# Third Strassen product by a second step, z added straight onto x1's buffer, and layer norm's squares on ScalarE: a two-layer graph kernel

## The chip, the cores and the metric

The kernel runs on one core of a Trainium2 chip. The metric is the device time of one launch in microseconds (us), the median of several runs. A core has five engines that run side by side: TensorE (PE, matrix products, into PSUM), VectorE (DVE), ScalarE (ACT), GpSimd (POOL) and SyncE (SP), which here issues the DMAs.

## The reference

64 graphs of 256 nodes with 512 features, two layers, everything in fp32:

```python
# layer 0:  x = layernorm(x + relu([x, (adj @ x) / max(deg, eps)] @ W.T))
# layer 1:  x = layernorm(x + softmax(w)[:, None] * (x @ Wv)),
#           w = q . (adj @ (k * mask)) / sqrt(512) * mask,  q, k = split(x @ Wqk)
def _layernorm(x, axis=-1, eps=1e-5):
    m = jnp.mean(x, axis=axis, keepdims=True)
    v = jnp.var(x, axis=axis, keepdims=True)
    return (x - m) / jnp.sqrt(v + eps)
```

(cut and joined; `deg` is the sum of a row of `adj`.) The kernel rewrites layer 0 as `x @ W_left` plus `adj @ (x @ W_right)` scaled by 1/deg, and folds Wq and Wk into one 512x512 matrix before the loop, so each layer has one product of x with 512x1024 weights and one product of adj with a 256x512 matrix (the "gather").

## The kernel before

Two graphs make a pair, j = 0 to 31. Iteration j works on layer 0 of pair j and, between its steps, on layer 1 of pair j-1. The product with the weights is done by a Strassen (Winograd) scheme with seven products P1 to P7; P1, P2 and P5 are themselves done by a second Strassen step of seven smaller products (`inner`), the others by plain accumulated matmuls (`outer`, `pairs`). All pieces are cut into units, and the program's order on TensorE is a string of unit names.

```python
    def inner(p, X, sides, w, q, done=lambda fifth: None):
        [...]
        lo, hi = w[:, :HF], w[:, HF:]              # two halves of a PSUM bank; HF = 256
        def first_two():
            mm(hi, s(0), b["T1"], start=True)
            mm(lo, X.chunk(block, 0, 0), b["B11"])
            act.copy(q[0][:, :HF], lo)
            tick()
        def second():
            mm(lo, s(1), b["T2"])                  # accumulates on lo: after the copy has read it
            act.copy(q[0][:, HF:], lo)
            tick()
        def third():
            mm(lo, s(2), b["T3"])
            act.copy(q[1].rearrange("p (h f) -> p h f", h=2), lo[:, None, :].to_broadcast([P, 2, HF]))
            fifth.append(small.tile([P, HF], F32, name="fifth", bufs=3))
            act.copy(fifth[0], hi)
            mm(q[0][:, :HF], X.chunk(block, 0, 1), b["B21"])
            tick()
        def last_two():
            mm(q[1][:, :HF], X.chunk(block, 1, 1), b["T4"])
            mm(q[0][:, HF:], s(3), b["B22"])
            [...]
```

Four calls of `inner`'s list are four steps: two matmuls, one, two, two. Side work (norms, softmax, sums for the next pair) is put in lists, `chains`; `tick()` at the end of each unit takes from them what fits by a clock that counts 0.43 or 0.86 us for each matmul and an assumed cost for each VectorE and ScalarE instruction. The clock does not know of DMAs. So each engine's order is fixed when the program is built.

```python
    def tick():
        while not quiet[0]:
            for c in list(chains):
                if c[2][0] <= clock[0] and c[3][0][0].free <= clock[0] + room[c[3][0][0]]:
                    step(c)
                    break
            else:
                return
[...]
    def degrees(j):
        [...]
        def degree(k, t):                           # r: the rows of adj, tile "turn"
            act.activation(r[:, k, t], r[:, k, t], AF.Copy, accum_out=deg[:, k, t:t + 1])
```

The tile `turn` has one buffer. It holds in turn the 32x32 blocks of x1 on their way through DMAs into the transposed `x1T`, and the rows of adj of the next pair, of which `degrees` makes the sums. `place` issues the 16 DMAs for x1T once the last norm of the pair before is done, then x and the rows are loaded by the same queue.

Of the kernel before, what the change touches and what calls it, by code (L numbers as in the profile page):

```python
# [50 lines left out]
class Side:  # L52
# [3 lines left out]
    def __init__(self, pool, name, home=None):  # L56
        self.pool, self.name = pool, name
        home = pool.tile([P, 2 * N_SIDE], F32, name=name) if home is None else home
        self.a = home.rearrange("p (k u e v n) -> p k u e v n", k=2, u=2, e=2, v=2)
        self.s = self.i = None  # L60

    def open_sums(self):
        self.s = self.pool.tile([P, 2, 4, 2, P], F32, name=self.name + "_s")
        self.i = self.pool.tile([P, 4, 3, P], F32, name=self.name + "_i")

    def block(self, s, ks):
        return self.s[:, ks, s] if isinstance(s, int) else self.a[:, ks, s[0], :, s[1]]

    def chunk(self, s, k, e):
        return self.s[:, k, s, e] if isinstance(s, int) else self.a[:, k, s[0], e, s[1]]  # L70
# [24 lines left out]
def resnorm_kernel(  # L95
# [104 lines left out]
    def load_xT(j, home=None):  # L200
        Xs[j] = Side(pool, "xT", home)
# [54 lines left out]
    def weight_sums(w, name):  # L256
# [4 lines left out]
        it = const.tile([P, 3, 3, HF], F32, name=f"{name}i")  # L261
        sides = {"B22": b22, "T2": t2, "T3": b12, "T4": t4}
        sub = lambda *args: lambda: vec.tensor_sub(*args)

        def inner_of(n, p, b):
# [5 lines left out]
                + [sub(b12, b22, b12), sub(t4, b21, t2)] + inner_of(1, "P2", b21))  # L271
# [3 lines left out]
    def outer_sums(X, eng, ks=slice(0, 2)):  # L275
        if X.s is None:
# [4 lines left out]
                (eng, lambda: eng.tensor_sub(a(S3), a(A11), a(A21))),  # L281
                (eng, lambda: eng.tensor_sub(a(S4), a(A12), a(S2)))]
# [5 lines left out]
    def inner_sums(X, eng, part):  # L288
# [3 lines left out]
        ks, b = ((slice(0, 2), X.first_row), (slice(2, 3), lambda k, e: X.s[:, k, S1:S1 + 1, e]))[part]  # L292
# [36 lines left out]
    def inner(p, X, sides, w, q, done=lambda fifth: None):  # L329

        n, block = {"P1": (0, A11), "P2": (1, A12), "P5": (2, S1)}[p]
# [25 lines left out]
        def last_two():  # L357
            mm(q[1][:, :HF], X.chunk(block, 1, 1), b["T4"])
            mm(q[0][:, HF:], s(3), b["B22"])
            if p != "P2":  # L360
# [30 lines left out]
    def gather(a, w, dst, u, p5, p2):  # L391
        r11, r12, r21, r22 = (dst[:, :, t, h * HF:(h + 1) * HF] for t in range(NT) for h in range(2))
# [8 lines left out]
        def u1():  # L401
            twice(u, "A11", "B11")
            act.copy(r11, of(u))
            tick()

        def g2():
            twice(p2, "A12", "B21")
            vec.tensor_add(r11, of(p2), r11)
# [22 lines left out]
        def u4():  # L431
            twice(u, "A22", "T4", start=False)
            act.copy(r21, of(u))
            tick()
        return dict(a=[u1], b=[g2], c=[g5], d=[u2], e=[u3], f=[g3], g=[u4])


# [21 lines left out]
    def norm0(j):  # L459
# [4 lines left out]
        x1Ts[j] = Side(pool, "x1T")  # L464
        sq = []

        def scaled(k, t):
            o = own[:, k, t]
            vec.scalar_tensor_tensor(o, z[:, k, t], rdeg[:, k, t:t + 1], o, op0=OP.mult, op1=OP.add)

        def residual(k, t):
            o = own[:, k, t]
            vec.scalar_tensor_tensor(o, o, 0.0, xs[j][:, k, t], op0=OP.max, op1=OP.add)
# [14 lines left out]
        for k in range(2):  # L488
            mv = small.tile([P, NT, 2], F32, name="mv")
            stats, scale = layer_norm(own[:, k], mv, NT)  # L490
# [396 lines left out]
```

## Time and profile before

| | |
|---|---|
| time, median of 3 | 1900.72 us (1900.2 to 1901.08) |
| span of the profiled run | 1898.0 us |
| ScalarE copies bank to bank, 128x256 / 128x512 | 384 of 363 ns / 192 of 585 ns |
| ScalarE scaling of the norms, 128x512 | 256 of 808 ns |
| VectorE norm statistics, 128x512, and their aggregate | 256 of 676 ns and 256 of 182 ns |
| VectorE adds bank + SBUF, 128x512 | about 680 ns |
| GpSimd sums for x and x1 | 0.45 to 1.6 us |

The page gives the busy time of each engine and the chain of work that ended last. Lists of groups give one line for each kind of instruction with its count, busy time and mean. A timeline line has start, duration, engine, source line, operation, output and input, shape and count; brackets give the idle time before it and what ended it. All instructions are recorded through two helper lines (L90 and L173), so tiles tell them apart. TensorE runs each fp32 matmul as two passes, so a count of x2 is one matmul.

### The profile page before, as it was taken

What the parts mean: (1) busy time and instruction counts of PE and PEld (TensorE: products, weight loads), DVE (VectorE), ACT (ScalarE), POOL (GpSimd) and SP (SyncE); (2) the same over time, 40 slices, a digit from 0 to 9 for tenths busy, and PEclk for the clock granted to TensorE, in tenths of its full rate; (3) what the DMA queues carried; (4) which work ended last, traced back from release to release, by engine and by line L of the source; (5) the groups of instructions that cost most, each with busy time, mean ns of one, the idle gap of its engine ahead of it and who ended that gap; (6) DMA issues with size and microseconds to landing.
All of it is one profiled execution on the core that took longest, in us unless ns stands there. A gap on an engine that the chain in (4) does not pass through costs nothing.

```text
span 1898.0 us, 22655 instructions
## 1 busy us (share of the span) xinstructions
PE 1875.2 (99%) x6596; PEld 1246.5 (66%) x6596; DVE 1588.2 (84%) x2952; ACT 1061.1 (56%) x2571; POOL 752.3 (40%) x898
## 2 busy tenths in 40 slices
PE   9999999999999999999999999999999999999997
PEld 5656666667666666666676666666666666666764
DVE  7788988888987889888889888898888898888886
ACT  3546555556555565554565655655555656555654
POOL 4444423444324434235444244343244442344421
PEclk9999999999999999999999999999999999999999
DMA  6333343442343433443433434334434334344321
GB/s 223 78 73 80 96 104 92 99 117 74 100 107 73 117 82 96 104 96 92 118 75 97 106 74 116 86 98 107 103 76 117 80 94 106 85 105 106 82 58 51
DMA packets 389147, 182.17 MB, mean 96 GB/s; under 512 B 272160, under 2 KB 353696, under 8 KB 389024
## 3 DMA queue, kind: packets, MB, share of 16 engines
q1 hardware_dynamic: 389024, 180.72, 36.7%
q8 instruction: 54, 0.88, 0.2%
q14 instruction: 69, 0.57, 0.1%
HBM read 114.10 MB, written 34.06 MB: 78 GB/s over the span
## 4 chain that ended last, share of the span: by engine, by line
PE 91%; DVE 4%; DMA 1%; SPq 1%; POOL 1%; issue 1%; ACT 0%; ACTq 0%; DVEq 0%; POOLq 0%
PE bank L173 91%; DVE own L90 1%; SPq L178 1%; DMA w<-w_t 1%; DVE st L90 1%; DVE y L90 0%; DVE tv L90 0%; DMA xT<-x_t 0%; DVE t_i L90 0%; DVE bank L90 0%; POOL xT_i L90 0%; POOL sa L90 0%; ACT own L90 0%; DMA turn<-adj 0%; POOL xT_s L90 0%
## 5 line engine op out<-in xcount | busy, mean ns | idle before, releaser
L90 ACT COPY bank<-bank 128x256 f32<-128x256 f32 (+1 forms) x576 | 252.0, 437 | 240.4 <-PE bank L173 231.4
L90 POOL TENSOR_TENSOR xT_i<-xT 128x256 f32<-128x256 f32 x62 | 58.9, 950 | 524.5 <-DMA xT<-x_t 490.0
L173 PE MATMUL bank<-w,x1T_s 128*128 128x512 f32 x512 | 260.4, 592 | 0.0
L173 PE MATMUL bank<-w,xT_s 128*128 128x512 f32 x512 | 230.2, 592 | 1.0 <-DVE y L90 1.0
L90 POOL TENSOR_TENSOR x1T_i<-x1T 128x256 f32<-128x256 f32 x64 | 51.2, 799 | 396.9 <-DMA x1T<-turn 383.0
L90 ACT ACTIVATE own<-own,shift,rstd 128x512 f32<-128x512 f32 x256 | 197.7, 808 | 14.1 <-DVE shift L90 13.8
L173 PE MATMUL bank<-tv,sa 128*128 128x256 f32 x768 | 191.9, 379 | 0.0
L173 PEld LDWEIGHTS bank<-tv,sa 128*128 128x128 f32 x768 | 145.8, 190 | 47.4 <-issue 16.0
L90 ACT COPY y<-bank 128x512 f32<-128x512 f32 x192 | 109.0, 587 | 119.9 <-PE bank L173 116.5
L90 DVE TENSOR_TENSOR y<-bank,y 128x512 f32<-128x512 f32 x192 | 128.5, 683 | 56.7 <-ACT y L90 53.0
L90 DVE BATCH_NORM_STATS2 st<-own 128x6 f32<-128x512 f32 x256 | 173.0, 676 | 2.4
L173 PE MATMUL bank<-t,xT_s 128*128 128x512 f32 (+1 forms) x384 | 158.6, 522 | 2.9 <-ACT own L90 2.9
L173 PEld LDWEIGHTS bank<-w,xT_s 128*128 128x128 f32 x512 | 97.2, 190 | 96.4 <-issue 85.8
L173 PE MATMUL bank<-t,x1T_s 128*128 128x512 f32 (+1 forms) x384 | 158.2, 521 | 0.3 <-ACT y L90 0.3
L90 ACT ACTIVATE turn<-turn 128x256 f32<-128x256 f32 x128 | 52.6, 411 | 169.2 <-DMA turn<-adj 169.2
L90 DVE TENSOR_TENSOR bank<-bank,fifth 128x256 f32<-128x256 f32 x256 | 97.0, 425 | 41.8 <-PE bank L173 41.8
L90 ACT COPY agg<-bank 128x512 f32<-128x512 f32 x128 | 74.4, 581 | 95.3 <-PE bank L173 94.0
L173 PE MATMUL bank<-t,x1T 128*128 128x512 f32 x256 | 125.2, 592 | 0.0
L173 PE MATMUL bank<-t,xT 128*128 128x512 f32 x248 | 121.6, 592 | 0.0
L90 POOL TENSOR_TENSOR sa<-adj 128x256 f32<-128x256 f32 x128 | 108.7, 849 | 26.8 <-ACT adj L90 20.9
L173 PE MATMUL bank<-t_i,x1T_i 128*128 128x256 f32 x384 | 114.4, 380 | 0.7 <-POOL x1T_i L90 0.4
L173 PE MATMUL bank<-t_i,xT_i 128*128 128x256 f32 x384 | 114.5, 380 | 0.2
(144 smaller groups left out, 4171.3 us busy)
## 6 DMA issues: line engine op xcount, KB each, us to landing
x<-x SPq DMA_DIRECT2D x64, 512.0 KB, 4.7
xT<-x_t SPq DMA_DIRECT2D x62, 512.0 KB, 6.2
x1T<-turn SPq DMA_DIRECT2D x496, 64.0 KB, 2.3
out<-own SPq DMA_DIRECT2D x62, 512.0 KB, 5.0
adj<-adj_t SPq DMA_DIRECT2D x64, 256.0 KB, 2.9
turn<-adj SPq DMA_DIRECT2D x64, 256.0 KB, 4.9
row<-d SPq DMA_DIRECT2D x31, 256.0 KB, 4.9
wqk<-wqk_t SPq DMA_DIRECT2D x4, 512.0 KB, 5.5
```

Source lines behind the costliest of these rows:

```text
L90: return self.tc.keep_in_program_order(getattr(self.engine, name)(out, *args, **kwargs))
L173: tc.keep_in_program_order(nc.tensor.matmul(ps, a, b, start=start, stop=True, skip_group_check=True))
L178: return tc.keep_in_program_order(nc.sync.dma_start(out, in_))
```

## The change

Three things are changed together. First, P3 of both layers is done by `inner` as well. It works on the sum S4, whose own small sums have to be made (`fourth_sums`, on GpSimd), whose result starts afresh in the PSUM banks y, so that what stood in y is added to the output before, and which has a fifth term to add afterwards. To save SBUF, S4 lies in the slot of a sum that is no longer read (S1 in layer 0, S2 in layer 1). Second, half of the gathered z of layer 0 is multiplied by 1/deg and added onto `own` (which becomes x1) straight from PSUM by VectorE; the tile z is half as large. Third, the norm's mean comes from an accumulated sum of the VectorE operation before it, and the variance from a Square with accumulation on ScalarE, in place of VectorE's statistics. The order strings are changed to fit. The core of the diff:

```diff
@@ -53,21 +52,22 @@
 
 
 
-    def __init__(self, pool, name, home=None):
+    def __init__(self, pool, name, over, home=None):
         self.pool, self.name = pool, name
+        self.slot = (0, 1, 2, over)
         home = pool.tile([P, 2 * N_SIDE], F32, name=name) if home is None else home
         self.a = home.rearrange("p (k u e v n) -> p k u e v n", k=2, u=2, e=2, v=2)
         self.s = self.i = None
 
     def open_sums(self):
-        self.s = self.pool.tile([P, 2, 4, 2, P], F32, name=self.name + "_s")
+        self.s = self.pool.tile([P, 2, 3, 2, P], F32, name=self.name + "_s")
         self.i = self.pool.tile([P, 4, 3, P], F32, name=self.name + "_i")
 
     def block(self, s, ks):
-        return self.s[:, ks, s] if isinstance(s, int) else self.a[:, ks, s[0], :, s[1]]
+        return self.s[:, ks, self.slot[s]] if isinstance(s, int) else self.a[:, ks, s[0], :, s[1]]
 
     def chunk(self, s, k, e):
-        return self.s[:, k, s, e] if isinstance(s, int) else self.a[:, k, s[0], e, s[1]]
+        return self.s[:, k, self.slot[s], e] if isinstance(s, int) else self.a[:, k, s[0], e, s[1]]
 
     def first_row(self, k, e):
 
[...]
@@ -278,8 +278,13 @@
         a = lambda s: X.block(s, ks)
         return [(eng, lambda: eng.tensor_add(a(S1), a(A21), a(A22))),
                 (eng, lambda: eng.tensor_sub(a(S2), a(S1), a(A11))),
-                (eng, lambda: eng.tensor_sub(a(S3), a(A11), a(A21))),
-                (eng, lambda: eng.tensor_sub(a(S4), a(A12), a(S2)))]
+                (eng, lambda: eng.tensor_sub(a(S3), a(A11), a(A21)))]
+
+    def fourth_sums(X):
+
+        ks = slice(0, 2)
+        gp.tensor_sub(X.block(S4, ks), X.block(A12, ks), X.block(S2, ks))
+        inner_sums(X, gp, 2)
 
     def run_now(steps):
         for _, work in steps:
[...]
@@ -328,7 +334,7 @@
 
     def inner(p, X, sides, w, q, done=lambda fifth: None):
 
-        n, block = {"P1": (0, A11), "P2": (1, A12), "P5": (2, S1)}[p]
+        n, block = {"P1": (0, A11), "P2": (1, A12), "P5": (2, S1), "P3": (0, S4)}[p]
         b = sides[p]
         s = lambda r: X.i[:, r, n]
         lo, hi = w[:, :HF], w[:, HF:]
[...]
@@ -357,7 +363,7 @@
         def last_two():
             mm(q[1][:, :HF], X.chunk(block, 1, 1), b["T4"])
             mm(q[0][:, HF:], s(3), b["B22"])
-            if p != "P2":
+            if p in ("P1", "P5"):
                 for k in range(2):
                     vec.tensor_add(q[k][:, HF:], q[k][:, HF:], fifth[0])
             done(fifth[0])
[...]
@@ -388,8 +394,18 @@
         vec.tensor_sub(t4, b21, t2)
         return {"B11": b11, "B21": b21, "B22": b22, "T1": t1, "T2": t2, "T3": t3, "T4": t4}
 
-    def gather(a, w, dst, u, p5, p2):
-        r11, r12, r21, r22 = (dst[:, :, t, h * HF:(h + 1) * HF] for t in range(NT) for h in range(2))
+    def gather(a, w, dst, u, p5, p2, own=None, rdeg=None):
+
+        if own is None:
+            r11, r12, r21, r22 = (dst[:, :, t, h * HF:(h + 1) * HF] for t in range(NT) for h in range(2))
+        else:
+            r12, r22 = dst[:, :, 0], dst[:, :, 1]
+
+        def onto(t, ps):
+            for k in range(2):
+                r = own[:, k, t, :HF]
+                vec.scalar_tensor_tensor(r, ps[:, k * HF:(k + 1) * HF], rdeg[:, k, t:t + 1], r,
+                                         op0=OP.mult, op1=OP.add)
 
         def twice(ps, s, b, start=True):
             for k in range(2):
[...]
@@ -430,10 +452,36 @@
 
         def u4():
             twice(u, "A22", "T4", start=False)
-            act.copy(r21, of(u))
+            if own is None:
+                act.copy(r21, of(u))
+            else:
+                onto(1, u)
             tick()
         return dict(a=[u1], b=[g2], c=[g5], d=[u2], e=[u3], f=[g3], g=[u4])
 
+
+    def norm_of(src, total):
+
+        rstd, shift, less, var = (small.tile([P, NT], F32, name=x) for x in ("rstd", "shift", "less", "var"))
+
+        def mean():
+            vec.tensor_scalar(less, total, -1.0 / F, None, op0=OP.mult)
+
+        def square(t):
+            junk = small.tile([P, F], BF16, name="junk", bufs=1)
+            act.activation(junk, src[:, t], AF.Square, bias=less[:, t:t + 1], accum_out=var[:, t:t + 1])
+
+        def factor():
+            act.activation(rstd, var, AF.Ln, bias=eps, scale=1.0 / F)
+            act.activation(rstd, rstd, AF.Exp, scale=-0.5)
+
+        def shifts():
+            vec.tensor_tensor(shift, less, rstd, op=OP.mult)
+
+        def scale(t):
+            act.activation(src[:, t], src[:, t], AF.Identity, bias=shift[:, t:t + 1], scale=rstd[:, t:t + 1])
+        return [(vec, mean)] + [(act, lambda t=t: square(t)) for t in range(NT)] + [(act, factor), (vec, shifts)] + [
+            (act, lambda t=t: scale(t)) for t in range(NT)]
 
     def layer_norm(src, mv, n):
 
[...]
@@ -486,13 +535,13 @@
                      sq[0][a * Q:(a + 1) * Q, b].rearrange("p k c t q -> p (k c t) q"))
         places[0] = place
         for k in range(2):
-            mv = small.tile([P, NT, 2], F32, name="mv")
-            stats, scale = layer_norm(own[:, k], mv, NT)
+            total = small.tile([P, NT], F32, name="sum")
             work = []
             for t in range(NT):
-                work += [(vec, lambda k=k, t=t: scaled(k, t)), (vec, lambda k=k, t=t: residual(k, t)), stats[t]]
+                work += [(vec, lambda k=k, t=t: scaled(k, t)),
+                         (vec, lambda k=k, t=t, total=total: residual(k, t, total))]
             turns = [(vec, lambda k=k, t=t: turn(k, t)) for t in range(NT)] if j < NP - 1 else []
-            queue(1, "norm", *work, *scale, *turns)
+            queue(1, "norm", *work, *norm_of(own[:, k], total), *turns)
 
     def scale_scores(j, to):
         vec.scalar_tensor_tensor(to, scores.pop(j), inv_scale, mask_sb[:, 2 * j:2 * j + 2, :],
[...]
@@ -601,8 +652,11 @@
         def after_p4(k):
             act.copy(own[:, k, 1], u[k])
 
-        def after_p3(k):
-            vec.tensor_add(yt[:, k, 0], y[k], yt[:, k, 0])
+        def after_p3(fifth):
+            for k in range(2):
+                vec.tensor_add(yt[:, k, 0], y[k], yt[:, k, 0])
+            add_fifth(yt[:, :, 0, HF:], fifth)
+
         def after_p5(fifth):
             pass
         return after_p1, after_p2, after_p3, after_p4, after_p5, after_p6, after_p7
[...]
@@ -632,7 +686,8 @@
 
         def after_p5(fifth):
             for k in range(2):
-                vec.tensor_add(vs[j][k][:, 1], y[k], vs[j][k][:, 1])
+                for t in (1, 0):
+                    vec.tensor_add(vs[j][k][:, t], y[k], vs[j][k][:, t])
 
         def after_agg():
             for k in range(2):
[...]
@@ -641,8 +696,11 @@
         def after_p4(k):
             dot(u[k], k, 1)
 
-        def after_p3(k):
-            vec.tensor_add(vs[j][k][:, 0], y[k], vs[j][k][:, 0])
+        def after_p3(fifth):
+            for k in range(2):
+                v = vs[j][k][:, 0]
+                vec.tensor_add(v, y[k], v)
+                vec.tensor_add(v[:, HF:], v[:, HF:], fifth)
         return after_p1, after_p2, after_p3, after_p4, after_p5, after_p6, after_p7, after_agg
 
     def pairs(ps, X, slot, b, done):
[...]
@@ -685,24 +744,27 @@
         k = inner("P5", X, W0, pw[1], y, a5)
         m = inner("P2", X, W0, pw[0], o, a2)
         p, q = pairs(u, X, S2, W0["T2"], a6), pairs(u, X, S3, W0["T3"], a7)
-        r, s = pairs(y, X, S4, W0["B22"], a3), pairs(u, X, A22, W0["T4"], a4)
+        r, s = inner("P3", X, W0, pw[1], y, a3), pairs(u, X, A22, W0["T4"], a4)
         if j == 0:
             run("i k i k i k i k", i=i, k=k)
             flush("degrees")
             load_rows(1)
         elif j == 1:
             run("i k i k i k i k", i=i, k=k)
+            fourth_sums(X)
             run("m p p m p p m", m=m, p=p)
             flush("norm")
             places[0](range(16))
         else:
-            run("i f k", i=i, k=k, f=open1)
+            run("i k", i=i, k=k)
             send_scores(j - 2)
-            run("i f k", i=i, k=k, f=open1)
+            run("i l k", i=i, k=k, l=open1)
             flush("norm")
             fetch_scores(j - 2)
             places[0](range(16))
-            run("i f k i f k", i=i, k=k, f=open1)
+            run("i k i k", i=i, k=k)
+        if j != 1:
+            fourth_sums(X)
         if j > 0:
             flush("mask")
             sumsM[j - 1] = adj_sums(j - 1)
[...]
@@ -714,51 +776,49 @@
             shared[0] = 1.0
         if j != 1:
             run("m p p m p p m", m=m, p=p)
-        run("q q q q m", m=m, q=q)
+        run("q q q", q=q)
+        flush("w0")
+        run("r q r m r s r", m=m, q=q, r=r, s=s)
         if j > 0:
             Y = x1Ts.pop(j - 1)
             inner_sums(Y, gp, 0)
             sums_Y = (*outer_sums(Y, vec), (vec, lambda: inner_sums(Y, gp, 1)))
         if j > 1:
             queue(1, "sums", *sums_Y)
-        run("r r r r", r=r)
         T = sums_T(ys[j])
 
         if j != 1 and j < NP - 1:
             degrees(j + 1)
-        zs[j] = pool.tile([P, 2, NT, F], F32, name="z")
-        g = gather(sumsA.pop(j), T, zs[j], pw[1], y[1], y[0])
-
-        def load_next():
+        zs[j] = pool.tile([P, 2, NT, HF], F32, name="z")
+        g = gather(sumsA.pop(j), T, zs[j], pw[1], y[1], y[0], owns[j], rdegs[j])
+
+        def sums_next():
             if j == NP - 1:
                 return
-            if j > 0:
-                load_xT(j + 1)
-                shared[0] = 1.25
             inner_sums(Xs[j + 1], gp, 0)
             rest = outer_sums(Xs[j + 1], gp)
             run_now(rest[:1])
             inner_sums(Xs[j + 1], gp, 1)
             late_sums.extend(rest[1:])
         if j == 0:
-            load_next()
+            sums_next()
             held = [c for c in chains if c[1] == "w1"]
             chains[:] = [c for c in chains if c[1] != "w1"]
-            run("s s a b c d s e s g f", s=s, **g)
+            run("s s s a b c d e g f", s=s, **g)
         else:
             u2, o2, y2 = o, pf, y
             b1, b2, b3, b4, b5, b6, b7, b8 = layer1(j - 1, ys[j][:, :, 0], o2, u2, y2)
             jj = inner("P1", Y, W1, pw[0], u2)
             k = inner("P2", Y, W1, y[0], o2, b2)
             if j == 1:
-                run("s s a b c d s e s g f", s=s, **g)
+                run("s s s a b c d e g f", s=s, **g)
                 flush("w1")
                 queue(1, "sums", *sums_Y)
                 run("j k j k j k j", j=jj, k=k)
                 b1(None)
                 run("k", k=k)
             else:
-                run("s s j a b s j c d s j e k j", s=s, j=jj, k=k, **g)
+                run("s s j s a b j c d j k e j", s=s, j=jj, k=k, **g)
                 quiet[0] = True
                 run("k", k=k)
                 quiet[0] = False
[...]
@@ -773,18 +833,22 @@
             g = gather(sumsM.pop(j - 1), T, aggs[j - 1], pw[0], o2[1], o2[0])
             h, q = pairs(u2, Y, S2, W1["T2"], b6), pairs(u2, Y, S3, W1["T3"], b7)
             n = inner("P5", Y, W1, pw[1], y2, b5)
-            p, open1 = pairs(u2, Y, A22, W1["T4"], b4), pairs(y2, Y, S4, W1["B22"], b3)
+            p, open1 = pairs(u2, Y, A22, W1["T4"], b4), inner("P3", Y, W1, pw[1], y2, b3)
             norm0(j)
             mask_adj(j)
             run("k h h" if j > 1 else "h h", k=k, h=h)
             if j == 1:
                 degrees(2)
                 flush("degrees")
-            load_next()
-            run("n k" if j > 1 else "n", k=k, n=n)
-            run("h h a n b q d q n c q e q p n g p f p", h=h, n=n, q=q, p=p, **g)
+            if j < NP - 1:
+                load_xT(j + 1)
+            run("n k h h" if j > 1 else "n h h", k=k, n=n, h=h)
+            fourth_sums(Y)
+            shared[0] = 1.25
+            sums_next()
+            run("a n b q d q n c q e q n p g f", n=n, q=q, p=p, **g)
             b8()
-            run("p", p=p)
+            run("p l p l p l", p=p, l=open1)
             py, pu = pu, py
         else:
             norm0(0)
[...]
```

Left out: the sums of b22 for P3 among the weights' sums (four more per layer, once), the same two steps of `onto` in g2, the same norm at layer 1's end, and the last pair behind the loop, whose P3 becomes `inner` in the same way.

## The prediction

> **What bounds the kernel now.** I read the page's busy shares first, then its chain that ended last, then ScalarE's waits, then the timeline of one pair of graphs.
>
> ```profile
> PE 1875.2 (99%) x6596; PEld 1246.5 (66%) x6596; DVE 1588.2 (84%) x2952; ACT 1061.1 (56%) x2571; POOL 752.3 (40%) x898
> ...
> PE 91%; DVE 4%; DMA 1%; SPq 1%; POOL 1%; issue 1%; ACT 0%; ACTq 0%; DVEq 0%; POOLq 0%
> ```
>
> TensorE is busy for 99% of the span and carries 91% of the chain; the others are hidden. In the timeline a 256-column matmul takes 0.43 us to the next one and a 512-column one 0.86, so I count in units of 0.431 us (256 columns). One pair j in the middle is 134 units, 57.8 us; the timeline agrees: from 171.5 to 1732.5 us there are 27 pairs, 57.8 us each. TensorE therefore has no slack to lose, and every engine that it waits for counts at once. Where is that nearest?
>
> ```profile
> ACT turn L90 <- DMA turn<-adj: 169.2, 29, 7.0
> ```
>
> This line of ScalarE's waits says: 29 times, once for each pair from 2 to 30, ScalarE stands still for 5.8 us on average until the rows for the degree sums land. Its queue is in order, so a PSUM copy queued behind them stands too. The timeline shows what follows (the pair at 576 us, TensorE then ScalarE):
>
> ```profile
> 603.36 1.02 PE L173 MATMUL bank<-t,xT 128*128 128x512 f32 x2
> 604.78 0.67 PE L173 MATMUL bank<-t_i,x1T_i 128*128 128x256 f32 x2 [0.40 <-POOL x1T_i L90]
> ...
> 602.58 0.42 ACT L90 ACTIVATE turn<-turn 128x256 f32<-128x256 f32 x1 [7.04 <-DMA turn<-adj]
> 602.90 0.19 ACT L90 ACTIVATION_READ_ACCUMULATOR turn<-turn 128x1 f32 x1
> 603.00 0.40 ACT L90 ACTIVATE turn<-turn 128x256 f32<-128x256 f32 x1
> 603.30 0.19 ACT L90 ACTIVATION_READ_ACCUMULATOR turn<-turn 128x1 f32 x1
> 603.39 0.56 ACT L90 COPY own<-bank 128x512 f32<-128x512 f32 x1
> 603.86 0.42 ACT L90 ACTIVATE turn<-turn 128x256 f32<-128x256 f32 x1
> 604.18 0.19 ACT L90 ACTIVATION_READ_ACCUMULATOR turn<-turn 128x1 f32 x1
> 604.27 0.37 ACT L90 COPY bank<-bank 128x256 f32<-128x256 f32 x1
> ```
>
> The second step of layer 1's P1 (604.78) overwrites the half bank that the copy at 604.27 empties, and starts 0.14 us after that copy's end at 604.64. The profile names GpSimd as the releaser, but in two other pairs (257.60 and 720.64 us) the same matmul also starts 0.14 us after the same copy, with GpSimd still busy. Call L the start of the first degree sum, measured from the pair's first matmul. Over the 29 pairs L is 24.0 to 26.5, mean 25.2. The copy ends at L + 2.1; TensorE wanted it at 28.0. So only pairs with L over 25.8 stall, and by tenths: three do. The kernel before sits just short of an edge.
>
> **What the Trainium skill says.** "PSUM — Partial Sum Buffer", section "Engine vs sequencer instructions": ScalarE's and VectorE's queues are strict FIFO. The stretch above agrees (the copy of a bank long full waited for the DMA). "ScalarE: Activation LUTs", section "What ACT_TABLE_LOAD costs": an ACTIVATE takes 186 ns + 0.833 ns per element of a row, about 93 ns more for each per-partition pointer operand, and neighbours overlap by about 93 ns. The trace agrees: the norm's scaling with two pointers should be 799 ns and is 808, the mask with one 492 against 514. "SBUF — State Buffer", section "SBUF: two separate sides": a VectorE operation with two SBUF inputs and a GpSimd one lock each other out. The trace fits: y times agg, both in SBUF, takes 685 to 1745 ns, bank times agg about 690.
>
> **The change, part by part.**
> *TensorE.* P3 was 4 matmuls of 512 columns = 8 units; as an inner product it is 7 of 256 = 7 units. Two layers, 32 pairs: 64 x 0.431 = 27.6 us less. A pair becomes 132 units, 56.9 us. Alone this makes 1873 us, and no other part of the change can take more from the chain.
> *ScalarE.* Squares: 252 of 128x512 with one pointer, an estimate from that page 186 + 93 + 427 = 706 ns, plus an accumulator read of 0.19 (as behind turn): +226 us. Inner copies: 128 x 0.363 + 64 x 0.585 + 64 x 0.375 = +108. Half of z no longer copied: 64 x 0.588 = -38. Sum +296, so 1357 us, 73%.
> *VectorE.* Statistics gone: 252 x (0.676 + 0.182) = -216. Accumulator reads of the 252 sums +35. z straight from the bank: 192 x about 0.4 = +77; then shorter scaling, fewer z adds and no S4: about -45 - 24 - 23. The product P3 starts afresh, so the earlier y must be added first: 64 y and 62 v adds x 0.683 = +86, and its fifth term +44. Sum near -66, about 1520 us, 81%.
> *GpSimd.* S4 (33 x 1.4) and 256 small sums of 0.5 to 0.9: about +200, so 950 us, 51%.
> On shares alone all of this is hidden. The waits decide.
>
> *The stretch around L in the new order.* From the order strings, a pair with j > 1 runs: i k i l k i k i k = 16 units; m p p m p p m = 13; q q q = 6; r q r m r s r = 13; s s j s a b j c d j k = 21; then e. The first j ends after 54 units, 23.3 us; the second wants to start after 60, at 25.9 (before: 28.0). TensorE comes here two microseconds earlier because three of four closing P3 steps went to the end of the pair before, one s moved up and P3 shrank. L does not move with it: it hangs on the last transposes of x1, 18 us earlier (582.54 to 583.25 in the timeline, 7.1 us after the first matmul), on 16 transposing DMAs, the x load and the load of the rows, all in the same order as before. I allow 0.2 us and take L = 25.0.
> ScalarE's stream there reads, in the changed program: turn turn turn, copy of j's first half bank, turn, own, square square, Ln Exp, copy of j's second, square square, copy of d (z). The new squares stand between copies that TensorE waits for. With steps from the timeline above (turn with its read 0.41, 256 copy 0.30 to the next start, 512 copy 0.50) and, for squares, 0.62 + 0.10, or 0.83 where the next waits for the sum:
> - first copy ends at L + 3 x 0.41 + 0.37 = L + 1.6; second j starts at L + 1.75 = 26.75, not 25.9.
> - second copy: L + 1.23 + 0.30 + 0.41 + 0.50 + 2 x 0.83 + 0.44 = L + 4.54 to L + 4.9; third j at 30.0.
> - copy of d: L + 4.54 + 0.30 + 0.83 + 0.72 = L + 6.4 to L + 7.0; e starts at L + 7.1 = 32.1.
> Unhindered, e would start after 69 units, at 29.7. The stall is 2.4 us per pair, of which 0.86 is paid by the two units saved: a pair takes 32.1 + 63 x 0.431 = 59.3 us, 1.5 more than before. For later copies of the pair I find slack of some tenths or more. Sum: 1900.7 + 29 x 1.45 = 1942.8; the pairs 0, 1 and 31 save 0.86 each, and the tail's fifth terms cost about 1: **1941 us**.
>
> **Rivals.** (1) *TensorE stays the bound*: the copies are served in time and 27.6 us come off: 1873 to 1880. For it: 0.4 us lost in a whole pair now, ScalarE at 73%. Against: L would have to be below 22.6 for e not to wait, and no pair shows under 24.0. For a gain it would have to be below 23.5. (2) *VectorE becomes the bound*: it now empties the gather's bank (u1 onto own) behind y adds, fifth and four tv sums. I get the bank free about 27.3, when d wants it at 27.1: 0.2 us per pair, under the shadow of ScalarE's stall. Alone: about 1880. (3) *GpSimd's S4 sums come late for P3*: they start when P5 has read S1 and need about 3.5 us; r comes 7 us later, so no wait; where SBUF locking doubles them, still none. (4) *The x^T load or the adj load is held by the first in, first out output DMA*: the last norm scale comes near the pair's end, but the adj load already waited for the last gather. No change.
>
> **Range and chances.** L's mean may be 0.5 off, worth 29 x 0.5 = 15 us; four squares off by 0.15 each, 17 us; some unseen wait adds, earlier ticks take away. That makes 1914 to 1966. The 2% line is 1938.7, nearly in the middle of it: slower by over 2% 0.52, within 2% 0.46, faster 0.02.
>
> **What would show it.** TensorE's busy share falls to about 96% with waits for ScalarE's bank and z copies of 2 to 2.5 us in each of 29 pairs, all between the first j and e; none elsewhere in the pair. Periods of 59.3 us from first matmul to first matmul. ScalarE near 1360 us, squares near 0.71 us, VectorE near 1520, GpSimd near 950. L about 25.0 from the first matmul. ScalarE's wait for turn should nearly keep its 169 us. If L is under 23.5, or if squares are sorted away from those copies by the time they run, the prediction is wrong and the time goes to 1880; if VectorE lags and delays the transposes, L grows and so does the time.

## The result and the profile after

The changed kernel takes **1961.08 us** (median of four runs, 1958.49 to 1962.88) beside 1900.57 us for the kernel before: a ratio of 1.0317, 95% interval 1.0299 to 1.0335. It is slower by over 2%, 20 us above the predicted 1941 and inside the range.

The page of the changed kernel, its busy line, its chain that ended last and the group of the new squares (busy us, mean ns, idle time before them and its releaser):

```profile
PE 1882.4 (96%) x6980; PEld 1310.1 (67%) x6980; DVE 1556.1 (79%) x3185; ACT 1304.8 (67%) x3267; POOL 896.1 (46%) x1187
...
PE 64%; SPq 11%; DMA 9%; ACT 7%; DVE 7%; issue 2%; POOL 0%; ACTq 0%; DVEq 0%
...
L90 ACT ACTIVATE junk<-own,less 128x512 bf16<-128x512 f32 x252 | 181.7, 721 | 62.4 <-DVE less L90 59.4
```

No engine beside TensorE is full: ScalarE, which got most of the new work, stands at 67%. But TensorE's part of the chain has gone from 91% to 64%, and the DMA queue, the DMAs and ScalarE have come in: the chain now runs over transfers and copies too. What TensorE waited for, in total, number of times and longest (us):

```profile
PE bank L173 <- ACT bank L90: 41.5, 60, 3.8
```

One middle pair shows where. It begins with its first matmul at 721.64 us; these are excerpts of ScalarE's and then TensorE's timeline:

```profile
746.46 0.42 ACT L90 ACTIVATE turn<-turn 128x256 f32<-128x256 f32 x1 [1.60 <-DMA turn<-adj]
...
747.67 0.36 ACT L90 COPY bank<-bank 128x256 f32<-128x256 f32 x1
...
748.38 0.56 ACT L90 COPY own<-bank 128x512 f32<-128x512 f32 x1
748.84 0.72 ACT L90 ACTIVATE junk<-own,less 128x512 bf16<-128x512 f32 x1
...
749.69 0.72 ACT L90 ACTIVATE junk<-own,less 128x512 bf16<-128x512 f32 x1
...
750.98 0.37 ACT L90 COPY bank<-bank 128x256 f32<-128x256 f32 x1
751.28 0.71 ACT L90 ACTIVATE junk<-own,less 128x512 bf16<-128x512 f32 x1
...
752.12 0.72 ACT L90 ACTIVATE junk<-own,less 128x512 bf16<-128x512 f32 x1
...
752.84 0.56 ACT L90 COPY z<-bank 128x512 f32<-128x512 f32 x1
...
748.38 0.59 PE L173 MATMUL bank<-t_i,x1T_i 128*128 128x256 f32 x2
748.81 2.13 PE L173 MATMUL bank<-tv,sa 128*128 128x256 f32 x8
...
751.49 0.67 PE L173 MATMUL bank<-w,x1T_i 128*128 128x256 f32 x2 [0.54 <-ACT bank L90]
...
753.45 1.13 PE L173 MATMUL bank<-tv,sa 128*128 128x256 f32 x4
```

The rows of adj land, the degree sums begin (746.46), and behind them in the queue stand two squares, the copy that j's third step needs (751.49 starts 0.14 us after that copy's end at 751.35), two more squares, and the copy of d's result, after which e starts at 753.45. Both copies could have gone earlier: by TensorE's records, whose ends are modelled, what they read was complete at 748.97 (j's second step) and 750.94 (d); they began at 750.98 and 752.84. Over the pairs 2 to 30 this gives the plainest sign of a cause: L, the start of the degree sums, varies from 23.9 to 27.0 us after the pair's first matmul, and the period (from one pair's first matmul to the next pair's) minus L is 34.23 to 34.25 us in 27 of the 29 pairs. There the period moves one for one with L.

The 60.7 us between the two profiled spans divide so:

| stretch | before | after | difference |
|---|---|---|---|
| start of the program to pair 2 | 113.0 | 128.8 | +15.8 |
| 29 periods, pair 2 to pair 31 | 57.83 each | 59.25 each | +40.9 |
| pair 31 to the end | 107.8 | 111.8 | +4.0 |

### The profile page after: what moved, and what is told of

The parts are those of the page before. It is cut to its first block, busy times and chain, and to the rows that moved or that the text cites. A ratio compares the mean times of both kernels' runs of the same rounds, so it can differ in the third digit from the quotient of the medians.

```text
span 1958.7 us, 24833 instructions
## 1 busy us (share of the span) xinstructions
PE 1882.4 (96%) x6980; PEld 1310.1 (67%) x6980; DVE 1556.1 (79%) x3185; ACT 1304.8 (67%) x3267; POOL 896.1 (46%) x1187
## 4 chain that ended last, share of the span: by engine, by line
PE 64%; SPq 11%; DMA 9%; ACT 7%; DVE 7%; issue 2%; POOL 0%; ACTq 0%; DVEq 0%
PE bank L173 64%; SPq L178 11%; DMA turn<-adj 6%; DMA x1T<-turn 3%; ACT junk L90 2%; ACT turn L90 2%; ACT bank L90 2%; DVE own L90 1%; DVE v L90 1%; DVE tv L90 1%; DVE y L90 1%; ACT own L90 1%; DVE turn L90 1%; ACT rstd L90 1%; DMA xT<-x_t 1%
## 5 line engine op out<-in xcount | busy, mean ns | idle before, releaser
L90 ACT COPY bank<-bank 128x256 f32<-128x256 f32 (+1 forms) x768 | 336.1, 438 | 218.1 <-PE bank L173 211.2
L90 ACT ACTIVATE junk<-own,less 128x512 bf16<-128x512 f32 x252 | 181.7, 721 | 62.4 <-DVE less L90 59.4
L173 PE MATMUL bank<-w,x1T_s 128*128 128x512 f32 (+1 forms) x384 | 168.3, 521 | 0.0
L90 POOL TENSOR_TENSOR x1T_i<-x1T_s 128x128 f32<-128x128 f32 x128 | 77.9, 608 | 188.8 <-DVE x1T_s L90 186.3
L90 DVE TENSOR_TENSOR v<-bank,v 128x512 f32<-128x512 f32 x186 | 119.1, 681 | 48.0 <-PE bank L173 48.0
L173 PE MATMUL bank<-w,xT_s 128*128 128x512 f32 (+1 forms) x384 | 153.6, 522 | 0.0
L173 PEld LDWEIGHTS bank<-t_i,x1T_i 128*128 128x128 f32 x512 | 95.6, 190 | 76.3 <-issue 67.6
L173 PEld LDWEIGHTS bank<-t_i,xT_i 128*128 128x128 f32 x512 | 95.3, 190 | 62.1 <-issue 50.9
L90 ACT COPY own<-bank 128x512 f32<-128x512 f32 x128 | 71.3, 582 | 95.4 <-PE bank L173 70.8
L173 PE MATMUL bank<-w,x1T_i 128*128 128x256 f32 x384 | 116.3, 385 | 17.7 <-ACT bank L90 14.7
```

The lines of the kernel that those rows point to most:

```text
L90: return self.tc.keep_in_program_order(getattr(self.engine, name)(out, *args, **kwargs))
L173: tc.keep_in_program_order(nc.tensor.matmul(ps, a, b, start=start, stop=True, skip_group_check=True))
```

## The experiments

The theory is that squares and copies stand in ScalarE's queue behind a wait for the rows' DMA. The rivals: ScalarE's load as such (244 us more of busy time, wherever it stands), VectorE, or the longer inner product with its copies. All ratios are to the kernel before.

**Squares taken back to VectorE (x_stats).** Part 3 undone, parts 1 and 2 kept:

```diff
-  sums and Squares of norm_of, in norm0 and finish
+  bn_stats and bn_aggr of layer_norm, as in the kernel before
```

> The changed kernel with the norm's statistics back on VectorE (no squares and no accumulated sums; all the rest of the change kept). Theory (four squares stand between copies that TensorE waits for, behind the wait for the rows): without them the copy of d is free in time, the pair falls from 59.2 to about 57.8 us (132 units plus the 0.9 us wait of P1's last step near 6 us of the pair, which stays), total about 1920 us. Rival A (the wait for the rows alone does it, squares or not): the pair stays near 59, total 1950 to 1961. Rival B (VectorE empties the gather's bank too late): VectorE gets about 7 us more work per pair, so the time stays or rises.

Measured: 1971.95 us (1.0371, 1.0341 to 1.0401), slower still: the theory and rival A missed, and rival B's case came. The period is 59.66. The waits for ScalarE at j's third step and at e are gone, though ScalarE still waits for the rows (57.7 us in 30 waits); but TensorE waits for VectorE instead. The line of TensorE's waits, then VectorE's and TensorE's timelines in one pair:

```profile
PE bank L173 <- DVE own L90: 35.4, 30, 2.2
```

```profile
686.90 0.68 DVE L90 BATCH_NORM_STATS2 st<-own 128x6 f32<-128x512 f32 x1
...
693.93 1.65 DVE L90 SCALAR_TENSOR_TENSOR own<-bank,rdeg,own 128x256 f32<-128x256 f32 x4
...
694.86 1.13 PE L173 MATMUL bank<-tv,sa 128*128 128x256 f32 x4 [1.06 <-DVE own L90]
```

Three statistics with their aggregates, 2.4 us from 686.90, stand ahead of the last additions into y, the four sums tv and the addition onto own that empties the gather's bank; the gather's d waits until its first half is through, by the starts of TensorE's records 1.3 us in a pair. Part 3 was therefore no ornament: without it parts 1 and 2 run into VectorE, though its busy share is 86% and its sum fits the pair.

**Squares without the wait (x_nowait).** The degree sums read rows that landed a pair ago. The rows are still loaded, but 1/deg then belongs to the pair before, so the output isn't the reference's.

```diff
-  act.activation(r[:, k, t], r[:, k, t], AF.Copy, accum_out=deg[:, k, t:t + 1])
+  act.activation(junk[:, :N], adjs[j - 1][:, k, t], AF.Copy, accum_out=deg[:, k, t:t + 1])
```

> The changed kernel, but from pair 3 on the degree sums read the transposed adj of the pair before, which landed long ago, in place of the rows that are just being loaded; the rows are still loaded, and the degrees are then those of other data. ScalarE's work and order are the same, only the wait for the DMA is gone. Theory: the first sum starts at about 24 us of the pair and not at 24.9 to 27, squares still stand before the copy of d; pair about 58.2 us, total about 1932. Rival A (the DMA wait alone): no stall is left but P1's last step, pair 57.8, total 1920. Rival C (ScalarE has too much work there, whatever it waits for): pair stays above 59, total 1955 or more.

Measured: 1921.6 us (1.0106, 1.0077 to 1.0135), period 57.93. All squares are there and as many instructions run; the waits between j and e are gone. It is not the load. The first degree sum started 23.1 us into the pair, earlier than the 24 expected, and the time is rival A's 1920 and not the theory's 1932. With x_stats this says that it takes both: without the wait the squares hold up nothing, and without the squares the wait holds up neither j's third step nor e.

**Degree sums later (x_defer).** They are queued behind layer 1's P2 and the gather's e, in front of "g f":

```diff
-  if j != 1 and j < NP - 1:        # ahead of the gather
-      degrees(j + 1)
   b1(None)
+  if j < NP - 1:
+      degrees(j + 1)
   run("g f", **g)
```

(pair 0 keeps its own call.)

> The changed kernel with the degree sums queued later, after layer 1's P2 and its e step, where nothing waits for them for half a pair; all data and results as in the reference. Theory: no PSUM copy stands behind the DMA and the squares get the free time before; pair about 57.8 us (0.9 us of it P1's last step), total about 1920. Rival C (ScalarE has too much work): pair above 59, total 1955. Rival B (VectorE late with the bank): d still waits, pair 58.5 or more.

Measured: 1921.16 us (1.0103, 1.0074 to 1.0133), period 57.93. The same gain by moving only the order and computing everything: 40 us. Both runs stay 1.0 us a pair above the 132 units of 0.431 us, and the reason is seen in the changed kernel's timeline too, ScalarE and then TensorE, 4 us into the pair:

```profile
725.56 1.52 ACT L90 ACTIVATE own<-own,shift,rstd 128x512 f32<-128x512 f32 x2
726.98 0.58 ACT L90 COPY bank<-bank 128x512 f32<-128x512 f32 x1
...
727.61 0.70 PE L173 MATMUL bank<-t_i,xT 128*128 128x256 f32 x2 [0.63 <-ACT bank L90]
```

Two scalings of the norm stand ahead of the copy that P1's last step waits for. Nothing here waits for a DMA: the new order strings put this step nearer to the flush of the norm. In the changed kernel this second loss adds nothing, since the period is set by L.

**Squares alone in the old order (b_squares).** The kernel before with part 3 only (the square's output goes to a tile that is dead by then):

```diff
-  stats, scale = layer_norm(own[:, k], mv, NT)      # VectorE
+  norm_of(own[:, k], total, dead)                   # sums on VectorE, Squares on ScalarE
```

> The kernel before with only the third part of the change: squares with accumulation on ScalarE in place of VectorE's statistics (their unused output goes to x or v, which nobody reads any more). Theory: in the old order the second step of layer 1's P1 comes 2 us later, and the squares fall behind the copies of z, so the pair stays at 57.8 to 58.2 us, total 1900 to 1912. Rival C (ScalarE has too much work with the squares): 1920 to 1950.

Measured: 1898.46 us (0.9983, 0.9976 to 0.9990), period 57.79. With the old strings the 252 squares cost nothing, and 0.17% is gained. Here ScalarE's timeline has the wait, the copy of z and, only 4.4 us later, the first square:

```profile
602.05 0.42 ACT L90 ACTIVATE turn<-turn 128x256 f32<-128x256 f32 x1 [6.48 <-DMA turn<-adj]
...
604.45 0.57 ACT L90 COPY z<-bank 128x512 f32<-128x512 f32 x1
...
608.81 0.73 ACT L90 ACTIVATE v<-own,less 128x512 f32<-128x512 f32 x1
```

They hurt where they are sorted in beside the wait.

**Rows loaded first (y_rows).** Only the DMA queue's order changes:

```diff
-  load_x(j)
   if j + 1 < NP:
       load_rows(j + 1)
+  load_x(j)
```

> The changed kernel with one thing moved: in each pair the rows of adj are loaded ahead of the rows of x, so that the degree sums can start earlier; the instructions of the compute engines are the same. Theory (the squares stand behind a wait of ScalarE for the rows): the first degree sum starts some 1.5 to 2 us earlier in the pair, at 23.0 to 23.5 us after the pair's first matmul instead of 24.9, and the squares and the copies behind them with it. If this wait sets the period alone, which was the first sum's start plus 34.3 us in the changed kernel, the period falls from 59.2 to about 57.8, and there stays the wait at the step that copies t into t_i (0.9 us a pair), which the rows have nothing to do with: about 1920 us. Rival (ScalarE's load of 296 more instructions is too much as such, wherever they stand): no change, 1961 us.

Measured: 1925.85 us (1.0129, 1.0114 to 1.0144). L falls from 24.9 to 23.3, the period to 58.1, and ScalarE waits for the rows for 6.2 us in all instead of 50.1 (the changed kernel's line, then this run's):

```profile
ACT turn L90 <- DMA turn<-adj: 50.1, 30, 3.7
```

```profile
ACT turn L90 <- DMA turn<-adj: 6.2, 9, 1.5
```

Degree sums that start 1.6 us earlier take 35 us off the time without touching a compute engine. That settles the steady part: the squares are late because the rows are.

**Both waits of the steady part (y_both).** The deferred sums, and the flush of the norm one step of P1 later:

```diff
   run("i k", i=i, k=k)
   send_scores(j - 2)
-  run("i l k", i=i, k=k, l=open1)
+  run("i k", i=i, k=k)
   flush("norm")
   [...]
-  run("i k i k", i=i, k=k)
+  run("i l k i k", i=i, k=k, l=open1)
```

> The changed kernel with two moves and no instruction more or less: the degree sums are queued behind layer 1's last gather step, after the copies that TensorE needs there, and the layer norm's scales are flushed one step of P1 later, behind the copy that the last step of P1 waits for. Theory (two waits of a TensorE that is otherwise busy): both stalls of 1.3 to 1.5 and 0.9 us are gone, the period is the 132 passes of 0.431 us, 56.9 us, or up to 57.1, and the time 1921 - 28 x 0.9 = about 1895 us; what the start and the end had lost, some 20 us, stays. Rival (removing one wait uncovers another just behind it, as when the sums of layer norm were put back on VectorE): the period stays at 57.5 or more, 1910 us or more.

Measured: 1952.72 us (1.0272, 1.0257 to 1.0288), period 58.92: worse than the deferral alone, and the rival's case. TensorE's timeline:

```profile
668.57 1.95 PE L173 MATMUL bank<-t,xT_s 128*128 128x512 f32 x4 [1.44 <-ACT own L90]
```

The later scalings made VectorE's transposes of the scaled tile wait 2.4 us in its queue, ahead of the additions on which a copy to own, and so the next product, waited. One edit of the order had moved the wait from ScalarE's queue to VectorE's, and made it longer.

**The start (y_w1) and all at once (y_best).** y_w1 moves w1's weight sums to GpSimd; y_best adds this to y_both, and leaves part of the closing work until after the last outputs:

```diff
-  queue(9, "w1", *[(vec, do) for do in work])
+  (the same sums on GpSimd, after fourth_sums of pair 1)
```

> The changed kernel with the sums of the blocks of w1 (needed once, for pair 1) moved from VectorE to GpSimd, behind the fourth sums of pair 1. Theory (the start loses its 16 us because VectorE has the weight sums ahead of the additions on which ScalarE's copies and so TensorE wait): the wait of 3.8 us at 83 us is gone, and with it part of the slow passes behind it: 5 to 10 us less before pair 2, the period unchanged at 59.2, about 1952 us. Rival (the start is lost in pair 0, by the gather's waits for the first weights' sums, before w1's sums come at all): 1959 to 1961 us.

> The two moves of the degree sums and of layer norm's scales, the sums of w1 on GpSimd, and the closing work of the last pair in two parts (the softmax and its additions before the last closes, the rest after them). If the four losses are independent: 1895 less 5 to 10 at the start and less 3 to 5 at the end, about 1883 us, 1% below the kernel before. If the losses hide one another or GpSimd's slower sums come late for pair 1: 1890 to 1900 us.

Measured: 1965.25 us (1.034, 1.0324 to 1.0355) and 1960.45 us (1.0312, 1.0295 to 1.0329). In y_w1 pair 1 began 1.8 us earlier, but pair 2 at 132.7 us instead of 128.8. The wait of 3.8 us at 83 us stayed (3.9 us, at 80), so taking w1's sums off VectorE did not remove it. GpSimd worked on w1 until 91.5 us, and beside that VectorE's four sums tv took 1.10 to 1.21 us each (0.68 to 0.69 in the changed kernel, where GpSimd stood idle). The gather's d waited longer for the addition onto own behind them. TensorE's line in the changed kernel, then in y_w1:

```profile
94.24 1.13 PE L173 MATMUL bank<-tv,sa 128*128 128x256 f32 x4 [0.45 <-DVE own L90]
```

```profile
94.05 2.07 PE L173 MATMUL bank<-tv,sa 128*128 128x256 f32 x4 [2.86 <-DVE own L90]
```

Then TensorE ran at half its clock until 104 us. y_best has y_both's period and y_w1's start, and the closing squares stood at the very end. With y_both these are three misses: work put out of one engine's way came to stand in another's.

**The scalings between copies (z_steady).** From here the moves were chosen by looking at which engine has a gap at that point:

```diff
   run("a n b q d q n c q e q n p g f", n=n, q=q, p=p, **g)
+  if j > 1:
+      early_shift()        # the second norm's shift, 0.15 us of VectorE, ahead of b8's products
   b8()
```

with the deferred sums, and the last but one pair's squares during the last products.

> The changed kernel with the degree sums behind layer 1's last gather step, as in x_defer (1921 us), and three instructions moved with none added: layer norm's second shift is issued ahead of the score products, so that the two scales behind it fall between copies of ScalarE instead of both ahead of the one that the last step of P1 waits for; and at the end of the program the squares of the last but one pair's outputs are issued during the last products instead of after them. Theory (x_defer still loses 0.9 us a pair to the pair of scales and some 4 us at the end to the squares): period 56.9 to 57.2 instead of 57.93, which is 20 to 29 us over 28 pairs, and 2 to 4 us at the end: 1889 to 1899 us, at or below the kernel before. Rival (as in y_both, the removed wait comes back at a later step because VectorE's transposes then hold up the additions): period 57.9 or more, 1917 us or more.

Measured: 1909.5 us (1.0031, 1.0019 to 1.0042), period 57.40. With its shift early, each scaling falls into one of ScalarE's gaps, and P1's last step no longer waits. The period is 0.2 us over the expected range: 0.39 us a pair is a wait of the gather for VectorE's addition onto own. The end became longer (113.9 us from pair 31 on, 111.9 in the changed kernel).

**The start in GpSimd's gap (z_all).** Half of w1's sums go where GpSimd stood idle for 12.6 us in pair 0, and in pairs 0 and 1 the addition onto own precedes the sums T3 and T4:

```diff
+  if j == 0:
+      (w1's first ten sums on GpSimd; the others after mask_adj(0))
-  run("s s s a b c d e g f", s=s, **g)
+  run("s s s a", s=s, **g)
+  T["rest"]()              # T3, T4
+  run("b c d e g f", **g)
```

> z_steady with the start changed: the sums of w1's blocks on GpSimd in pair 0, where GpSimd has 12 us of idle time, ahead of the sums for pair 1 and not behind them as in y_w1; in pairs 0 and 1 the third and fourth sum for the gather are issued after the addition that empties the gather's bank; and in pair 1 layer norm is flushed one step of TensorE later. Theory (the start is lost to VectorE's program order in pairs 0 and 1, and to the lower clock that follows each long wait of TensorE): pair 2 starts at 117 to 122 us instead of 128, so 6 to 11 us below z_steady. Rival (GpSimd and VectorE slow one another, or the sums of x1T come late again as in y_w1): no gain, pair 2 at 127 us or later.

Measured: 1902.78 us (0.9998, 0.9989 to 1.0006). Pair 2 began at 122.5 us, 6 less.

**Two last versions (z_final, z_last).** z_final puts w1's second half behind pair 1's own sums, gives the last but one pair VectorE's statistics again, and extends the order of z_all's gather to all pairs. z_last is z_final without that extension.

> z_all with its three remaining losses addressed: the second half of w1's sums on GpSimd stands behind the sums that pair 1 needs first and no longer ahead of them (z_all: TensorE waited 3.7 us for xT_s); in every pair the third and fourth sum for the gather follow the addition that empties the gather's bank (z_steady: 0.39 us a pair); and the outputs of the last but one pair, and they alone, have their sums of squares from VectorE's statistics again, as in the kernel before, so that the squares are not in the last products' way (pair 31 to the end: 107.7 us before, 111.9 in the changed kernel, 114.7 in z_all). Theory (the 27.6 us of matmul that P3 saves were used up by waits and by nothing else): period 57.0 to 57.2, 4 to 6 us less at the start, 5 to 7 at the end: 1881 to 1890 us, faster than the kernel before by 0.6 to 1%. Rival (each wait that is removed uncovers one nearly as long): 1898 us or more.

> z_final with one of its moves taken back from pair 2 on: the third and fourth sum for the gather stand ahead of the addition again, and only pairs 0 and 1 keep the other order. In z_final the start was 5.3 us shorter than in z_all (pair 2 at 117.2 instead of 122.5 us) but the period was 59.1 instead of 57.4 us, since the squares of the second half waited 1.5 and 2.0 us for VectorE ahead of the copies into agg. Theory (only that move did it): pair 2 at 117 us, 29 periods of 57.4, and 109 us from pair 31 to the end: 1891 us, 0.5% below the kernel before. Rival (another move of z_final did it): 1940 us.

z_final: 1944.18 us (1.0218, 1.0205 to 1.0232), a miss, with a period of 59.1. The scheduler sorted the squares anew; ScalarE's timeline of one pair shows them in front of the second gather's copies once more, this time waiting for VectorE:

```profile
694.34 0.72 ACT L90 ACTIVATE junk<-own,less 128x512 bf16<-128x512 f32 x1 [1.54 <-DVE less L90]
...
699.99 0.72 ACT L90 ACTIVATE junk<-own,less 128x512 bf16<-128x512 f32 x1 [1.96 <-DVE less L90]
...
701.55 0.56 ACT L90 COPY agg<-bank 128x512 f32<-128x512 f32 x1
```

By the starts of TensorE's records the waits in the second gather are 1.1 of the 1.8 us by which z_final's period exceeds z_last's. Another 0.5 us is a wait for VectorE's addition onto own at a step of layer 1's P1, since half of that addition now stands behind the two sums.

z_last: **1894.87 us** (0.9961, 0.9948 to 0.9975), 0.4% below the kernel before and 4 us above what was expected; period 57.32, pair 2 at 118.3 us. That one reordering did the damage, as the theory said. The page of z_last:

```profile
PE 1859.3 (98%) x6980; PEld 1313.1 (69%) x6980; DVE 1526.7 (81%) x3171; ACT 1298.2 (69%) x3259; POOL 907.2 (48%) x1207
...
PE 84%; DVE 12%; ACT 1%; issue 1%; POOL 1%; DMA 1%; SPq 0%; ACTq 0%; DVEq 0%
```

The products of the changed kernel and nearly the same side work, 66 us faster by order and placement. Of the 27.6 us that P3 saves, 15 appear in the periods (29 x 0.52); the start (118.3 instead of 113.0 us) and the end (110.2 instead of 107.8) take back 7.7, which leaves 7.3; the two medians, 1902.27 and 1894.87, are 7.4 apart.

## Why the prediction was right, and where not

The verdict was right, and for the reason given, but 20 us were missing. That it came out so clearly was luck: the prediction put 1941 us, 2 us over the 2% line at 1938.7, and gave the slower verdict 0.52. Without what it missed at the start and the end, the measured time would be 1940 us, next to that line as well.

- *TensorE's saving and what the others are given.* No engine became the bound by its sum. ScalarE came out 52 us under the predicted 1357, VectorE 36 over its 1520, GpSimd 54 under its 950. The squares' 706 ns, estimated from the Trainium skill's "ScalarE: Activation LUTs", section "What ACT_TABLE_LOAD costs", measured 721.
- *The edge at L.* Right. L has a mean of 24.92 (predicted 25.0). In the pair shown L is at 746.46: j's third step was worked out at L + 5.0 and started at L + 5.03; e at L + 7.1 and started at L + 6.99. Period 59.25 (predicted 59.3); stall per pair, by the starts of TensorE's records, 2.35 us (predicted 2.4). One of the three waits was not there in the pair shown: j's second step was to start 0.15 us behind its copy and starts 0.35 us behind it (748.03 to 748.38), since TensorE itself came late (next point); in pairs with a later L it does wait. x_nowait, x_defer and y_rows show that this wait is the cause, each from another side. The strict FIFO of the Trainium skill's "PSUM — Partial Sum Buffer", section "Engine vs sequencer instructions", is what carries it, and the trace agrees: the copy of d stood in ScalarE's queue for 1.9 us (750.94 to 752.84) while j's copy and two squares ahead of it ran.
- *"None elsewhere in the pair", "slack of some tenths or more" for later copies.* Wrong. 0.9 us of the 2.35 stood at P1's last step, behind the norm's scalings. I had worked through the copies around L only and not those around the flush of the norm, where ScalarE's work had not grown but TensorE's order had. It changed no total, since L is counted from the pair's first matmul and the wait fell inside L; but with the edge gone it costs 0.9 us a pair, 26 us in 29 pairs (x_defer). It also spoils a sign: the prediction put a gain, and 1880 us, at L under 23.5, but x_nowait with L at 23.1 had a period of 57.93 and took 1921.6.
- *Start and end.* The failed term of the sum. Pairs 0 and 1 were put at 0.86 us less each and the end at about the same (0.86 less in pair 31, 1 more for the fifth terms); measured +15.8 and +4.0. I counted their instructions, as in the middle. Pair 1 begins 9.5 us later than in the kernel before, and most of that lies between the gather's first matmul and pair 1: 15.7 us instead of 7.9. In pair 0 VectorE still makes the weights' sums, four more per layer, and its sums for the gather stand behind them; the new string puts the gather's steps in a row, with no other product between them to fill its waits; and part of it runs at half the clock (last section). z_all and z_last take 6 and 10.5 of the 15.8 us away by order and by what GpSimd takes over. How the rest divides, and which part each cause has, is not shown. The end: the closing squares in ScalarE's queue delay a shift of VectorE by 3.7 us, and 15.9 us lie behind the last matmul's start instead of 12.6.
- *ScalarE's wait for turn keeps its 169 us.* Wrong: 50.1 us in 30 waits. The wait is still there for the rows, but a copy to own, itself waiting for TensorE, now stands ahead of the sums and takes its time.
- *Rival 2, VectorE.* 0.2 us a pair was the right size as long as ScalarE has the squares (by the starts 0.14 in x_defer, 0.38 in z_steady); x_stats shows 1.3 without them. Rivals 1, 3 and 4 were rightly set aside for the middle; GpSimd was in TensorE's way for 2.7 us in all.

Not tried: the new order strings without the three parts; part 1 with the full tile z, since the half z makes room for it; and a scheduler that knows when the DMAs land.

## What to carry to other kernels

Saved matmuls count only if the copies that free the banks come earlier by as much: before adding work to a side engine, list for each copy TensorE waits for what stands ahead of it in its queue, and ask of each entry what that waits for, a DMA above all. A period minus the time of a suspected event that stays constant to hundredths while the event wanders by microseconds is worth more than any busy share. And treat the first two and the last iterations as programs of their own: their queues hold other work, and here they held a third of the loss.

## What the runs showed of the hardware

After some waits in the start TensorE's clock was halved. Windows of the changed kernel: stretch and length in us, TensorE's busy time in it, granted clock, DMA share and GB/s:

```profile
30.00:60.00 30.00, 24.80 (x73) 0.88 0.12 36
60.00:90.00 30.00, 26.12 (x83) 0.89 0.12 20
```

The first of these windows in the kernel before, with the busy time of TensorE, its weight loads, VectorE, ScalarE and GpSimd ahead of the clock:

```profile
30.00:60.00 30.00, 29.49 (x102) 18.68 (x101) 26.24 (x42) 13.56 (x36) 16.27 (x16) 1.00 0.12 36
```

In the changed kernel, from about 53 to 63 us, and again from 84 to 87, a 256-column pass takes 0.427 instead of 0.216 us to the next. The first spell follows waits of 1.4 and 2.2 us, the second one of 3.8 us. By the sum of the lengthened passes this is some 5 of the 15.8 us that the start lost. The Trainium skill's "TensorE: Matmul & The Clock Gate", section "What's actually happening", describes a clock halved after an idle window of some 3.4 us that runs freely; the doubled passes agree. So does what followed one and the same wait of 3.0 us in the starts of z_final (70.6 to 73.6 us) and z_last (70.0 to 73.1 us): no slow pass in z_final, 3.4 us at half clock in z_last. TensorE's windows there, z_final's and then z_last's:

```profile
73.80:77.00 3.20, 3.20 (x14) 1.00 0.65 103
```

```profile
73.10:74.00 0.90, 0.90 (x5) 1.00 0.46 74
74.10:77.40 3.30, 3.30 (x9) 0.50 0.51 80
```

But the first spell of the changed kernel had no single wait above 2.24 us. How much idle time is enough stays open.
